# Layer 1's second product as seven products over two super-tiles, issued from a slot list

## The chip, the cores and the metric

The kernel runs on one core of a Trainium2 chip. The metric is device time in microseconds (us) from start to end of one execution; the median of several runs is given. Engines are called by the profile's names: PE (TensorE, matmuls), PEld (its weight loads), DVE (VectorE), ACT (ScalarE), POOL (GpSimd), SP (SyncE, which here only issues transfers).

## The reference, cut to what matters

Four layers are applied to `x` of shape 128 x 64 x 256, each `x = x + layer(relu(layernorm(x)))`: a graph convolution with LSTM windows (layer 0), a normalised graph convolution with an MLP (layer 1), a three-matrix graph convolution (layer 2) and masked attention (layer 3). The change is in layer 1:

```python
agg = jnp.einsum('nm,bmd->bnd', A_hat, features)
x = agg.reshape(-1, d)                              # 8192 x 256
h = jax.nn.relu(_batchnorm(x @ W1.T + b1, g1, be1)) # first product, 8192 x 512
out = h @ W2.T + b2                                 # second product, 8192 x 256
out = _batchnorm(out, g2, be2)
```

A batchnorm needs the mean and variance of each channel over all 8192 rows. So nothing of the second product can start before the first product is done for every row, and nothing of the next layer before the second is.

## The kernel before, in words

The 8192 rows are cut into 16 super-tiles of 512 rows (`SUP = 512`, `NS = 16`). All is float32. In layer 1 the data lie channel-major: a tile holds 128 channels on the partitions and the 512 rows of a super-tile along the free axis. The hidden 512 channels are four such chunks (`HC = 4`), the output's 256 are two (`KC = 2`).

The kernel runs in stages: layer 0's graph part; the LSTM; `first_product`; `second_product`; and `rest`, which holds layers 2 and 3. Where a stage goes through super-tiles, `pipelined` advances the generators of several super-tiles by one step in turn, the newest first, and this order is the order of each engine's queue (`tc.manual_schedule()`). Each engine works through its queue in order; semaphores make it wait for data.

The steps that the change touches:

- `zslot(s, c)` is the place of chunk c of super-tile s of the hidden layer. Chunks 0 and 1 lie in the large buffers `hbuf` (`hS`, `hT`), chunks 2 and 3 in the tiles `zb` (called `z` in the profile). The second product writes its output over chunks 0 and 1.
- `first_product(s)` loads x, copies layer 0's result in row order with POOL (`hs`, L330), transposes it on PE (L203) and adds x, applies the layernorm (whose power is one POOL operation, L179), aggregates over the graph on PE (L193), multiplies by W1 on PE (L341), evicts with the bias on ACT (L343) and takes statistics on DVE (L346).
- `bn_coeffs` turns the statistics of all super-tiles into one scale and one shift per channel (L580 to L585).
- `second_product(s)`, before: ACT applies scale, shift and Relu to four chunks in place (L618); PE sums four matmuls into each of two banks (L626); DVE adds the bias on the way out of PSUM (L630) and takes statistics (L631). One super-tile's Relus stand a step ahead of its matmuls.
- `rest(s)` loads layer 1's input again (`x1`, L662), applies the second batchnorm's coefficients to y (L665) and transposes back (L203).

The LSTM already uses a seven-product form. Each gate over two blocks of 512 columns is a 2 x 2 by 2 x 2 block product in seven products instead of eight, with three PSUM banks "a", "b" and "c", of which "a" is evicted and then accumulated into further. Its work is a list of events `at(t, fn, ...)`, sorted by t and issued in that order; t counts slots of PE time. The weight sums that the form needs come from `weight_sums`, on POOL; the input sums from DVE (`input_sums`, L385), the state sums from DVE or POOL (`state_sums`, L405 to L408). The weights lie in a tile of seven blocks, the last three or four of them made from the first four.

Of the kernel before, what the change touches and what calls it, by code (L numbers as in the profile page):

```python
# [9 lines left out]
F32 = mybir.dt.float32  # L10
AF = mybir.ActivationFunctionType
ALU = mybir.AluOpType
AX = mybir.AxisListType

P = 128
# [5 lines left out]
def kernel(ctx: ExitStack, tc: tile.TileContext, a: dict, out: bass.AP):  # L21
# [4 lines left out]
    nc = tc.nc  # L26
# [4 lines left out]
    KC = D // P  # L31
    SUP = 512
    NS = NT // SUP
# [6 lines left out]
    HC = H1 // P  # L40
# [27 lines left out]
    def bank():  # L68
        return psum.tile([P, 512], F32, tag="ps", name="ps")
# [12 lines left out]
    def weight(name, src, pool=const):  # L82
        k, m = src.shape
        return load_const(name, src.rearrange("(c p) m -> p c m", p=P), [P, k // P, m], pool)
# [24 lines left out]
    bn2 = load_const("bn2", a["bn2"], [P, 3, KC])  # L109
# [87 lines left out]
    def to_token_major(src, add, dst):  # L197

        for q2 in range(0, Q, 2):
            p_ = bank().rearrange("p (q d) -> p q d", q=2)  # L200
            for q in range(2):
                for c in range(KC):
                    nc.tensor.transpose(p_[:, q, ts(c, P)], src(c, q2 + q), ident)  # L203
            nc.vector.tensor_add(dst[:, q2 : q2 + 2, :], add[:, q2 : q2 + 2, :], p_)
# [6 lines left out]
    def place(s):  # L211
        return hbuf[s // SG], (s % SG) * SUP
# [7 lines left out]
    def pipelined(gens, skew, live=()):  # L220

        gens, live, r = list(gens), list(live), 0
        with tc.manual_schedule():
            while gens or live:
                if gens and r % skew == 0:
                    live.insert(0, gens.pop(0))
                live = [g for g in live if next(g, "end") != "end"]
                r += 1  # L230
# [12 lines left out]
    OF = (None, A11, A12, S4, A22, S1, S2, S3)  # L243
# [9 lines left out]
    def weight_sums(w):  # L253
        g = nc.gpsimd
        g.tensor_add(w[:, S1], w[:, A21], w[:, A22])
        g.tensor_sub(w[:, S2], w[:, S1], w[:, A11])
        g.tensor_sub(w[:, S3], w[:, A11], w[:, A21])
        g.tensor_sub(w[:, S4], w[:, A12], w[:, S2])
# [60 lines left out]
    def zslot(s, c):  # L319

        g, c0 = place(s)
        return g[:, c, c0 : c0 + SUP] if c < KC else zb[s][:, c - KC, :]

    def first_product(s):
        xt = pb[0].tile([P, Q, D], F32, tag="xt", name="xt")
        nc.sync.dma_start(xt, x_r[s])
        hs = pb[0].tile([P, KC * SUP], F32, tag="hs", name="hs")
        hsT = hs.rearrange("p (c n) -> p c n", c=KC)
        for c in range(KC):
            nc.gpsimd.tensor_copy(hsT[:, c, :].rearrange("p (b t) -> p b t", t=T), graphs(s, c))  # L330
        yield
        to_token_major(lambda c, q: hsT[:, c, ts(q, P)], xt, xt)
        nc.sync.dma_start(x1d[s], xt)
        h = layernorm_relu(lns, xt, h=hs.rearrange("p (q d) -> p q d", q=Q))
        yield
        ag = aggregate(pb[0], h, ahT, "ag", 2)
        yield
        for o in range(HC):
            p_ = bank()
            for c in range(KC):  # L340
                nc.tensor.matmul(p_, w1[:, c, ts(o, P)], ag[:, c, :],  # L341
                                 start=(c == 0), stop=(c == KC - 1))
            nc.scalar.activation(zslot(s, o), p_, AF.Identity, bias=bn1[:, 0, o : o + 1])  # L343
        yield
        for o in range(HC):
            nc.vector.bn_stats(st1[:, o, s, :], zslot(s, o))  # L346
        yield
# [7 lines left out]
    events = []  # L355

    def at(t, fn, *args):
        events.append((t, len(events), fn, args))
# [169 lines left out]
    t = 0.0  # L528
    wt[0][0].append(wih0[0])
    for p in range(1, NL + 1):  # L530
# [8 lines left out]
        for k in range(0, len(pairs), 2):  # L539
            sts = [{"blk": blk, "N": blk[0][2] * GB, "p": p, "pool": pool}  # L540
                   for blk, pool in zip(pairs[k : k + 2], (lh0, lh1))]
            for j in range(p):
                for st in sts:
# [4 lines left out]
                    t = step(t, st, j, j == p - 1, l, wt[l], turn)  # L548
# [40 lines left out]
    hbuf = [spare.tile([P, KC, GRP], F32, tag="hS", name="hS"), *hT]  # L589

    with tc.tile_pool(name="pz", bufs=1, reuse_waits="tile") as pz:
        w2 = weight("w2", a["W2T"], pz)
        zb = [pz.tile([P, HC - KC, SUP], F32, tag=f"z{s}", name=f"z{s}") for s in range(NS)]
        st1 = pz.tile([P, HC, NS, 6], F32, tag="st1", name="st1")
        st2 = pz.tile([P, KC, NS, 6], F32, tag="st2", name="st2")

        gens = [*early, *(first_product(s) for s in range(3, NS))]
        with tc.manual_schedule():
            next(gens[3])
            next(gens[0])  # L600
        pipelined(gens[4:], 1, gens[3::-1])
        front.close()
        last.close()
        late = ctx.enter_context(tc.tile_pool(name="late", bufs=1, side="right", reuse_waits="tile"))
        wl2 = [weight(f"wl2_{k}", a["W"][k], late) for k in range(3)]
        bl2 = row_bcast("bl2", a["bias"], D, late)
        wqk = late.tile([P, KC, D], F32, tag="wqk", name="wqk")
        wvo = late.tile([P, KC, D], F32, tag="wvo", name="wvo")
        products = ExitStack()
        wt = products.enter_context(tc.tile_pool(name="wt", bufs=1, reuse_waits="tile"))  # L610
        wqkv = weight("wqkv", a["Wqkv"], wt)
        wo = weight("wo", a["Wo"], wt)
        co1 = bn_coeffs(pz, st1, HC, bn1, "bn1")

        def second_product(s):
            for c in range(HC):
                z = zslot(s, c)
                nc.scalar.activation(z, z, AF.Relu, bias=co1[:, 1, c : c + 1],  # L618
                                     scale=co1[:, 0, c : c + 1])
            yield  # L620
            acc = []
            for o in range(KC):
                p_ = bank()
                acc.append(p_)
                for c in range(HC):
                    nc.tensor.matmul(p_, w2[:, c, ts(o, P)], zslot(s, c),  # L626
                                     start=(c == 0), stop=(c == HC - 1))
            for o in range(KC):
                y = zslot(s, o)
                nc.vector.tensor_scalar_add(y, acc[o], bn2[:, 0, o : o + 1])  # L630
                nc.vector.bn_stats(st2[:, o, s, :], y)  # L631
            yield

        pipelined(map(second_product, range(NS)), 1)
        co2 = bn_coeffs(pz, st2, KC, bn2, "bn2")

        with tc.manual_schedule():
            wT = wt.tile([P, 3 * KC, D], F32, tag="wT", name="wT")  # L640
            for k in range(3):
                p_ = bank().rearrange("p (d c) -> p d c", d=KC)
                for d in range(KC):
                    for c in range(KC):
                        nc.tensor.transpose(p_[:, d, ts(c, P)], wqkv[:, c, ts(k * KC + d, P)], ident)
                nc.scalar.copy(wT[:, k * KC : (k + 1) * KC, :], p_)
            for left, right, to in ((0, wT[:, KC : 2 * KC, :], wqk), (2, wo, wvo)):
                p_ = bank().rearrange("p (c m) -> p c m", c=KC)
                for c in range(KC):
                    for d in range(KC):  # L650
                        nc.tensor.matmul(p_[:, c, :], wT[:, left * KC + d, ts(c, P)],
                                         right[:, d, :], start=(d == 0), stop=(d == KC - 1))
                nc.scalar.copy(to, p_)
        products.close()


    with tc.tile_pool(name="pc", bufs=2, reuse_waits="tile") as pc, tc.tile_pool(name="pc1", bufs=1, reuse_waits="tile") as pc1:

        def rest(s):
            g, c0 = place(s)  # L660
            x1 = pc.tile([P, Q, D], F32, tag="x1", name="x1")
            nc.sync.dma_start(x1, x1d[s])  # L662
            y = g[:, :, c0 : c0 + SUP]
            for c in range(KC):
                nc.vector.tensor_scalar(y[:, c, :], y[:, c, :], co2[:, 0, c : c + 1],  # L665
                                        co2[:, 1, c : c + 1], op0=ALU.mult, op1=ALU.add)
            yield
            x2 = pc.tile([P, Q, D], F32, tag="x2", name="x2")
            to_token_major(lambda c, q: y[:, c, ts(q, P)], x1, x2)


            h = layernorm_relu(pc, x2)
# [4 lines left out]
            for c in range(KC):  # L677
                for q2 in range(0, Q, 2):
                    half = [bank()[:, : 6 * T].rearrange("p (q k n) -> p q k n", q=2, k=3)
                            for _ in range(2)]  # L680
                    for q in range(2):
                        for b in range(2):
                            r = slice(b * T, (b + 1) * T)
                            nc.tensor.matmul(half[b][:, q], h[r, q2 + q, ts(c, P)], adj3[r, :, r],  # L684
                                             start=True, stop=True)
                    for b in range(2):
                        copy = nc.vector.tensor_copy if b else nc.scalar.copy
                        to = ag[:, c, :, q2 * P : (q2 + 2) * P].rearrange("p k (q n) -> p q k n", q=2)
# [3 lines left out]
            for q2 in range(0, Q, 2):  # L692
                p_ = bank().rearrange("p (q d) -> p q d", q=2)
                for q in range(2):
                    for n in range(3 * KC):
                        c, k = divmod(n, 3)
                        nc.tensor.matmul(p_[:, q, :], ag[:, c, k, ts(q2 + q, P)], wl2[k][:, c, :],  # L697
                                         start=(n == 0), stop=(n == 3 * KC - 1))
# [6 lines left out]
            for c in range(KC):  # L705
                p_ = bank()
# [5 lines left out]
            for o in range(KC):  # L712
                p_ = bank()
                for c in range(KC):
                    nc.tensor.matmul(p_, wqk[:, c, ts(o, P)], h3T[:, c, :],  # L715
                                     start=(c == 0), stop=(c == KC - 1))
# [3 lines left out]
            p_ = bank()  # L720
            for q in range(Q):
                for c in range(KC):
                    nc.tensor.matmul(p_[:, ts(q, P)], qk[:, c, ts(q, P)], h3T[:, c, ts(q, P)],  # L723
                                     start=(c == 0), stop=(c == KC - 1))
# [76 lines left out]
```

## Time and profile before

| what | value |
|---|---|
| time, median of 3 runs | 1948.85 us (1948.57 to 1951.17) |
| span of the profiled run | 1946.4 us |
| PE busy | 1900.9 us (98%) |
| DVE busy | 1071.7 us (55%) |
| ACT busy | 830.3 us (43%) |
| POOL busy | 506.2 us (26%) |
| granted PE clock, mean | 0.996 |
| second product's matmuls (L626) on the final chain | 111.83 us, from 1392.81 |

PE, PEld and the others are separate rows: a PE that is busy says that matmuls are in its pipeline, and the row PEld, the weight loads, overlaps it. The chain that ended last is followed backwards from the last instruction, at each step to what released it; time on it is time that the kernel's end depends on. A single f32 matmul of the program is two MATMUL records and two LDWEIGHTS records in this trace. "Idle before" tells how long an engine stood still ahead of an instruction and who released it.

### The profile page before, as it was taken

How to read it: one execution, taken by the hardware profiler on the slowest of the kernel's cores; microseconds unless marked ns; L12 is line 12 of the kernel's file. 1: busy time of each engine (PE TensorE's matmuls, PEld its weight loads, DVE VectorE, ACT ScalarE, POOL GpSimd, SP SyncE). 2: the span in 40 equal slices, each digit the busy share in tenths (PEclk: the TensorE clock that was granted, in tenths of full speed). 3: DMA queues.
4: the chain of work that ended last, by engine and by line, in shares of the span. 5: the costliest groups of instructions: out<-in, count | busy, mean ns of one | idle time of the engine just before them, and what ended most of it. 6: DMA issues, size and time to landing. Idle time of an engine off the chain costs nothing.

```text
span 1946.4 us, 19096 instructions
## 1 busy us (share of the span) xinstructions
PE 1900.9 (98%) x7092; PEld 1156.7 (59%) x7092; DVE 1071.7 (55%) x2108; ACT 830.3 (43%) x1398; POOL 506.2 (26%) x330
## 2 busy tenths in 40 slices
PE   7999999999999999999999999999999899999998
PEld 6776444444446666665444444555444678888887
DVE  6775777635447345345433334688544555556553
ACT  3554667534435335335433333344650243333332
POOL 1110322543324434322522224432000211111110
PEclk9999999999999999999999999999999999999999
DMA  5110000000001000000000001333000101111111
GB/s 156 55 33 1 1 1 26 19 0 0 0 0 44 1 1 1 1 1 22 0 0 1 1 0 54 109 109 117 11 0 21 34 1 44 44 44 44 44 33 44
DMA packets 48909, 54.29 MB, mean 28 GB/s; under 512 B 2992, under 2 KB 44208, under 8 KB 48816
## 3 DMA queue, kind: packets, MB, share of 16 engines
q1 hardware_dynamic: 44784, 49.29, 7.9%
q10 hardware_dynamic: 4032, 3.78, 0.7%
q8 instruction: 56, 0.92, 0.2%
q14 instruction: 37, 0.30, 0.1%
HBM read 36.28 MB, written 16.78 MB: 27 GB/s over the span
## 4 chain that ended last, share of the span: by engine, by line
PE 94%; DVE 2%; ACT 1%; POOL 1%; DMA 1%; issue 0%; DVEq 0%; POOLq 0%; ACTq 0%
PE ps L423 33%; PE ps L429 18%; PE ps L697 9%; PE ps L626 6%; PE ps L341 6%; PE ps L193 5%; PE ps L753 3%; PE ps L289 3%; PE ps L300 3%; PE ps L715 2%; PE ps L684 2%; PE ps L723 1%; PE ps L203 1%; PE ps L745 1%; PE ps L708 1%; DVE ln_st L176 0%
## 5 line engine op out<-in xcount | busy, mean ns | idle before, releaser
L445 DVE TENSOR_TENSOR gate<-gate,ps 128x512 f32<-128x512 f32 (+2 forms) x378 | 223.7, 619 | 456.9 <-PE ps L429 377.4
L423 PE MATMUL ps<-tx,wih 128*128 128x512 f32 (+2 forms) x1008 | 448.4, 544 | 6.0 <-ACT gate L448 4.0
L423 PE MATMUL ps<-hT,wih 128*128 128x512 f32 (+2 forms) x756 | 338.5, 541 | 0.0
L423 PEld LDWEIGHTS ps<-tx,wih 128*128 128x128 f32 x1008 | 191.1, 191 | 196.9 <-issue 133.7
L448 ACT COPY gate<-ps 128x512 f32<-128x512 f32 (+2 forms) x252 | 134.2, 533 | 378.5 <-PE ps L429 324.6
L441 ACT ACTIVATE gate<-gate,lbias 128x512 f32<-128x512 f32 (+2 forms) x252 | 216.7, 860 | 153.6 <-DVE gate L445 153.6
L429 PE MATMUL ps<-h,whh 128*128 128x512 f32 (+2 forms) x576 | 257.5, 529 | 0.0
L423 PEld LDWEIGHTS ps<-hT,wih 128*128 128x128 f32 x756 | 143.6, 190 | 142.1 <-issue 79.9
L179 POOL TENSOR_TENSOR ln_rn<-ln_rn,mhalf 128x4 f32<-128x4 f32 x64 | 64.7, 1010 | 522.9 <-DVE ln_rn L178 522.9
L429 PE MATMUL ps<-th,whh 128*128 128x512 f32 (+2 forms) x432 | 192.5, 527 | 0.0
L429 PEld LDWEIGHTS ps<-h,whh 128*128 128x128 f32 x576 | 109.7, 191 | 100.6 <-issue 76.9
L697 PE MATMUL ps<-wl,ag 128*128 128x256 f32 x768 | 168.4, 379 | 0.0
L697 PEld LDWEIGHTS ps<-wl,ag 128*128 128x128 f32 x768 | 144.7, 190 | 19.0
L468 POOL TENSOR_TENSOR gate<-gate 128x1024 f32<-128x1024 f32 (+2 forms) x36 | 71.9, 2019 | 309.6 <-ACT gate L441 309.6
L183 ACT ACTIVATE ln_h<-x,ln_rn 128x256 f32<-128x256 f32 x128 | 66.4, 589 | 189.4 <-DVE ln_rn L180 189.4
L468 POOL TENSOR_TENSOR cell<-gate 128x1024 f32<-128x1024 f32 (+2 forms) x36 | 79.4, 2225 | 200.1 <-ACT gate L441 200.1
L429 PEld LDWEIGHTS ps<-th,whh 128*128 128x128 f32 x432 | 82.2, 190 | 75.9 <-issue 58.1
L341 PE MATMUL ps<-ag,w 128*128 128x512 f32 x256 | 112.3, 592 | 0.0
L468 POOL TENSOR_TENSOR cell<-gate,cell 128x1024 f32<-128x1024 f32 (+2 forms) x32 | 65.1, 2052 | 103.6 <-ACT gate L441 103.6
L448 DVE COPY gate<-ps 128x512 f32<-128x512 f32 (+2 forms) x126 | 78.5, 623 | 21.6 <-PE ps L429 21.6
L441 ACT ACTIVATE gate<-ps,lbias 128x512 f32<-128x512 f32 (+2 forms) x126 | 79.5, 631 | 3.5 <-PE ps L429 0.5
L473 ACT ACTIVATE gate<-cell 128x1024 f32<-128x1024 f32 (+2 forms) x72 | 68.2, 952 | 27.8 <-POOL cell L468 27.8
(164 smaller groups left out, 2492.8 us busy)
## 6 DMA issues: line engine op xcount, KB each, us to landing
xt<-in_x_dram SPq DMA_DIRECT2D x31, 512.0 KB, 4.4
x1d<-xt SPq DMA_DIRECT2D x16, 512.0 KB, 3.0
x<-x1d SPq DMA_DIRECT2D x16, 512.0 KB, 4.5
out_dram<-x SPq DMA_DIRECT2D x16, 512.0 KB, 3.2
wih<-in_WihT_dram SPq DMA_DIRECT2D x16, 256.0 KB, 4.8
whh<-in_WhhT_dram SPq DMA_DIRECT2D x12, 256.0 KB, 4.7
wqkv<-in_Wqkv_dram ACTq DMA_DIRECT2D x1, 768.0 KB, 4.3
wl<-in_W_dram ACTq DMA_DIRECT2D x3, 256.0 KB, 3.2
```

The lines of the kernel that those rows point to most:

```text
L183: nc.scalar.activation(h[:, q, :], src[:, q, :], AF.Relu, bias=rn[:, 1, q : q + 1], scale=rn[:, 0, q : q + 1])
L193: nc.tensor.matmul(p_[:, ts(q, P)], h[:, q, ts(c, P)], mT, start=True, stop=True)
L341: nc.tensor.matmul(p_, w1[:, c, ts(o, P)], ag[:, c, :], start=(c == 0), stop=(c == KC - 1))
L423: nc.tensor.matmul(wide(p_[:, :N]), wih[0][:, OF[k], gi, :], x_, start=first_, stop=(j == 0), skip_group_check=True)
L429: nc.tensor.matmul(p_[:, :N], whh[0][:, OF[k], gi, :], h_, start=False, stop=True, skip_group_check=True)
L441: nc.scalar.activation(to, r[bank_][:, :N] if bank_ else to, fn, bias=lbias[:, l, m : m + 1])
L445: nc.vector.tensor_add(slot(n, hc), slot(n, hc), r[bank_][:, :N])
L448: op(slot(n, hc), r[bank_][:, :N])
L468: fn(*((t["G"] if isinstance(t, dict) and "G" in t else st["c"])[:, n, :, : st["N"]] for t in tiles))
L473: nc.scalar.activation(o_, c, AF.Tanh)
L626: nc.tensor.matmul(p_, w2[:, c, ts(o, P)], zslot(s, c), start=(c == 0), stop=(c == HC - 1))
L697: nc.tensor.matmul(p_[:, q, :], ag[:, c, k, ts(q2 + q, P)], wl2[k][:, c, :], start=(n == 0), stop=(n == 3 * KC - 1))
```

## The change

Two neighbouring super-tiles are taken together. With rows n = 0, 1 (the super-tile) and, for each half k of the hidden channels, two chunks c = 0, 1, the product of the two by the weights is a 2 x 2 by 2 x 2 block product, summed over k = 0, 1. It is computed with seven block products per k instead of eight. This takes four sums of the weights, made once by POOL at `s == 8` of the first product (`weight_sums(w2)`), and four sums of the hidden chunks (T1 to T4) for each pair and k: those of k = 0 on DVE, those of k = 1 on POOL. T3 is made in place, over chunk b12; the rest lie in a new pool `tp` with two buffers. Three banks per pair, "a", "b", "c", are used as in the LSTM's gates: "a" is evicted by ACT after product 1, accumulated into by 6, evicted again, accumulated into by 7, added by DVE to y(1,1), accumulated into by 4 and evicted at last.

All is put on a slot list. Pair i starts at slot 7i and its products stand at 7i + 0, 1, 3, 5, 9, 11 and 13, so two pairs interleave and every slot has one product of two matmuls. The four outputs are written over chunks that are no longer needed, which permutes them over the pair; `yslot` tells where each lies, for the statistics and for `rest`. The bias is now added by ACT on three of the outputs' evictions and on that of "a" into T2. W2's tile grows from four blocks of 256 columns to seven blocks of 2 x 128 and is loaded in four pieces from SP, where it was one transfer from ACT's queue.

```diff
+    def yslot(s, o):
+        n, c = {(0, 0): (0, 0), (1, 1): (0, 1), (1, 0): (1, 1), (0, 1): (1, 0)}[s % 2, o]
+        return zslot(s - s % 2 + n, c)
...
     def first_product(s):
         xt = pb[0].tile([P, Q, D], F32, tag="xt", name="xt")
+        if s == 8:
+            weight_sums(w2)
...
-        w2 = weight("w2", a["W2T"], pz)
+        w2 = pz.tile([P, 7, 2, P], F32, tag="w2", name="w2")
+        for o in range(2):
+            for c in range(2):
+                nc.sync.dma_start(w2[:, 2 * o + c], a["W2T"].rearrange(
+                    "(k c p) (o m) -> o c p k m", c=2, p=P, m=P)[o, c])
...
-        def second_product(s):
-            for c in range(HC):
-                z = zslot(s, c)
-                nc.scalar.activation(z, z, AF.Relu, bias=co1[:, 1, c : c + 1],
...
-                for c in range(HC):
-                    nc.tensor.matmul(p_, w2[:, c, ts(o, P)], zslot(s, c),
-                                     start=(c == 0), stop=(c == HC - 1))
-            for o in range(KC):
-                y = zslot(s, o)
-                nc.vector.tensor_scalar_add(y, acc[o], bn2[:, 0, o : o + 1])
-                nc.vector.bn_stats(st2[:, o, s, :], y)
...
+            def sums(name, k, engine):
...
+                b11, b21, b12, b22 = (z(n, 2 * k + c) for n in range(2) for c in range(2))
+                if name == "T1":
+                    engine.tensor_sub(tt["T1"][:, k], b12, b11)
+                elif name == "T2":
+                    engine.tensor_sub(tt["T2"][:, k], b22, tt["T1"][:, k])
+                elif name == "T3":
+                    engine.tensor_sub(b12, b22, b12)
+                else:
+                    engine.tensor_sub(tt["T4"][:, k], b21, tt["T2"][:, k])
...
+            for k, (n, c) in enumerate(((0, 1), (0, 3), (0, 0), (0, 2), (1, 0), (1, 2), (1, 1), (1, 3))):
+                at((-6.3, -5.8, -5.3, -4.4, -3.9, -3.4, -2.4, -1.9)[k], relu, n, c)
+            for k, engine in enumerate((nc.vector, nc.gpsimd)):
+                for name, t in (("T1", -2.8), ("T2", 0.1), ("T3", 0.6), ("T4", 1.6)):
+                    at(t, sums, name, k, engine)
+            for t, name, j in ((0, "c", 2), (1, "a", 1), (3, "b", 5), (5, "a", 6), (9, "a", 7),
+                               (11, "b", 3), (13, "a", 4)):
+                at(t, product, name, j)
+            at(2, lambda: evict(y(0, 0), 0, "a"))
+            at(3.1, lambda: add(y(0, 0), y(0, 0), "c"))
+            at(3.6, stats, 0, 0)
+            at(4, lambda: evict(y(1, 1), 1, "b"))
+            at(6, lambda: evict(tt["T2"][:, 0], 0, "a"))
+            at(10, lambda: add(y(1, 1), y(1, 1), "a"))
+            at(10.5, stats, 1, 1)
+            at(12, lambda: add(y(1, 0), tt["T2"][:, 0], "b"))
+            at(12.5, stats, 1, 0)
+            at(14.2, lambda: evict(y(0, 1), 1, "a"))
+            at(15, stats, 0, 1)
...
         def rest(s):
-            g, c0 = place(s)
...
-            y = g[:, :, c0 : c0 + SUP]
+            y = [yslot(s, c) for c in range(KC)]
```

More of the change, by code (lines that the diff above doesn't have):

```diff
@@ L613 @@
         co1 = bn_coeffs(pz, st1, HC, bn1, "bn1")
-        def second_product(s):
-            for c in range(HC):
-                z = zslot(s, c)
-                nc.scalar.activation(z, z, AF.Relu, bias=co1[:, 1, c : c + 1],
-                                     scale=co1[:, 0, c : c + 1])
-            yield
-            acc = []
-            for o in range(KC):
-                p_ = bank()
-                acc.append(p_)
-                for c in range(HC):
-                    nc.tensor.matmul(p_, w2[:, c, ts(o, P)], zslot(s, c),
-                                     start=(c == 0), stop=(c == HC - 1))
-            for o in range(KC):
-                y = zslot(s, o)
-                nc.vector.tensor_scalar_add(y, acc[o], bn2[:, 0, o : o + 1])
-                nc.vector.bn_stats(st2[:, o, s, :], y)
-            yield
@@ L634, with second_product, z, relu @@
-        pipelined(map(second_product, range(NS)), 1)
+        events = []
+        def second_product(i, tp):
+            t0 = 7.0 * i
+            tt, banks = {}, {}
+            def z(n, c):
+                return zslot(2 * i + n, c)
+            def relu(n, c):
+                nc.scalar.activation(z(n, c), z(n, c), AF.Relu, bias=co1[:, 1, c : c + 1],
+                                     scale=co1[:, 0, c : c + 1])
+            def sums(name, k, engine):
+                if name != "T3" and name not in tt:
+                    tt[name] = tp.tile([P, 2, SUP], F32, tag=name, name=name)
+                b11, b21, b12, b22 = (z(n, 2 * k + c) for n in range(2) for c in range(2))
[7 more added lines that the diff above has]
+                    engine.tensor_sub(tt["T4"][:, k], b21, tt["T2"][:, k])
+            def product(name, j):
+                new = name not in banks
+                if new:
+                    banks[name] = bank()
+                for k in range(2):
+                    x_ = (z(0, 2 * k), z(0, 2 * k + 1), z(1, 2 * k + 1),
+                          *(tt[v][:, k] if v in tt else None for v in ("T4", "T1", "T2")),
+                          z(1, 2 * k))[j - 1]
+                    nc.tensor.matmul(banks[name], w2[:, OF[j], k, :], x_, start=(new and k == 0),
+                                     stop=(k == 1), skip_group_check=True)
+            def evict(to, o, name):
+                nc.scalar.activation(to, banks[name], AF.Identity, bias=bn2[:, 0, o : o + 1])
+            def add(to, src, name):
+                nc.vector.tensor_add(to, src, banks[name])
+            def y(n, o):
+                return yslot(2 * i + n, o)
+            def stats(n, o):
+                nc.vector.bn_stats(st2[:, o, 2 * i + n, :], y(n, o))
+            def at(t, fn, *args):
+                events.append((t0 + t, len(events), fn, args))
+            for k, (n, c) in enumerate(((0, 1), (0, 3), (0, 0), (0, 2), (1, 0), (1, 2), (1, 1), (1, 3))):
[17 more added lines that the diff above has]
+            at(15, stats, 0, 1)
@@ L635 @@
+        with tc.tile_pool(name="tp", bufs=2, reuse_waits="tile") as tp:
+            for i in range(NS // 2):
+                second_product(i, tp)
+            with tc.manual_schedule():
+                for _, _, fn, args in sorted(events, key=lambda e: e[:2]):
+                    fn(*args)
         co2 = bn_coeffs(pz, st2, KC, bn2, "bn2")
@@ L659, in rest @@
         def rest(s):
-            g, c0 = place(s)
             x1 = pc.tile([P, Q, D], F32, tag="x1", name="x1")
             nc.sync.dma_start(x1, x1d[s])
-            y = g[:, :, c0 : c0 + SUP]
+            y = [yslot(s, c) for c in range(KC)]
             for c in range(KC):
-                nc.vector.tensor_scalar(y[:, c, :], y[:, c, :], co2[:, 0, c : c + 1],
-                                        co2[:, 1, c : c + 1], op0=ALU.mult, op1=ALU.add)
+                nc.vector.tensor_scalar(y[c], y[c], co2[:, 0, c : c + 1], co2[:, 1, c : c + 1],
+                                        op0=ALU.mult, op1=ALU.add)
             yield
             x2 = pc.tile([P, Q, D], F32, tag="x2", name="x2")
-            to_token_major(lambda c, q: y[:, c, ts(q, P)], x1, x2)
+            to_token_major(lambda c, q: y[c][:, ts(q, P)], x1, x2)
             h = layernorm_relu(pc, x2)
```

## The prediction

> **What bounds the kernel now.** I read the page's engine shares first, then the chain by line, the chain in order of time, and then only the stage that the change touches.
>
> ```profile
> PE 1900.9 (98%) x7092; PEld 1156.7 (59%) x7092; DVE 1071.7 (55%) x2108; ACT 830.3 (43%) x1398; POOL 506.2 (26%) x330
> PE 94%; DVE 2%; ACT 1%; POOL 1%; DMA 1%; issue 0%; DVEq 0%; POOLq 0%; ACTq 0%
> ```
>
> PE carries 94% of the chain that ended last, so a PE instruction removed counts in full unless a wait takes its place. The chain in order of time shows how much of it is this stage:
>
> ```profile
> 1374.22 13.75 PE ps L341 x32
> 1392.81 111.83 PE ps L626 x256
> 1506.24 3.72 PE ps L651 x16
> 1516.18 4.54 PE ps L684 x32
> ```
>
> L626, the second product, is one unbroken block of 111.83 us. Its 256 records are 128 matmuls of the program: each f32 matmul leaves two. The windows (us, PE, PEld, DVE, ACT, POOL, granted clock, DMA) split that block:
>
> ```profile
> 1392.00:1400.00 8.00, 7.19 (x13) 3.12 (x14) 0.79 (x2) 8.00 (x12) 0.00 (x0) 0.79 0.00 0
> 1400.00:1420.00 20.00, 20.00 (x48) 8.80 (x47) 8.10 (x12) 20.00 (x29) 0.00 (x0) 1.00 0.00 1
> 1420.00:1505.00 85.00, 85.00 (x203) 37.84 (x202) 36.74 (x52) 17.17 (x25) 0.00 (x0) 1.00 0.00 0
> ```
>
> From 1400 on PE never idles, at full clock; POOL does nothing, DVE is busy 45 of 105 us, and ACT, which runs ahead with its Relus, is done by 1438. Matmul starts in the timeline are 1.717 us apart for four records, 0.429 each. 256 x 0.429 = 109.9, so 1.9 us of the 111.83 are lost at the start. The timeline there:
>
> ```profile
> 1391.95 1.52 ACT L618 ACTIVATE hS<-hS,bn1co 128x512 f32<-128x512 f32 x2 [3.26 <-DVE bn1co L585]
> 1394.20 0.34 PEld L626 LDWEIGHTS ps<-hS,w 128*128 128x128 f32 x1 [0.40 <-issue]
> 1397.19 0.19 PEld L626 LDWEIGHTS ps<-z,w 128*128 128x128 f32 x1 [0.24 <-issue]
> ```
>
> PE comes out of a 4.9 us idle spell and loads weights at 0.34 us, half speed, until about 1396.8: that is the loss. At the end of the stage:
>
> ```profile
> 1504.76 0.75 DVE L630 TENSOR_SCALAR hT<-ps,bn 128x512 f32<-128x512 f32 x1 [0.47 <-PE ps L626]
> 1505.54 0.69 DVE L631 BATCH_NORM_STATS2 st<-hT 128x6 f32<-128x512 f32 x1
> ```
>
> Behind these come the statistics, the coefficients and the first transposes of the last stage. PE's filler (L645, L651) lies beside them.
>
> **What the Trainium skill says.** "TensorE: Matmul & The Clock Gate", section What's actually happening: PE's clock is halved when idle and needs about 3.4 us of work to warm; the trace agrees (0.34 against 0.19 us for about 4 us). "SBUF — State Buffer", section Who interferes with whom: a VectorE instruction with two SBUF inputs contends with a GpSimd instruction that reads SBUF. The trace agrees: the L385 subtractions below go from 0.69 to 2.85 us. "PSUM — Partial Sum Buffer", section The four PSUM rules: a matmul without the first flag adds onto what the bank holds, which is what reusing bank "a" after an eviction rests on; the gates at L423 do the same here.
>
> **Prices.** From the traced lines (min/median/max) and groups (busy us, mean ns):
>
> ```profile
> L343 ACT ACTIVATE z<-ps,bn x32: 669/676/687, 1248.8 to 1388.0; 128x512 f32<-128x512 f32 x32
> L385 DVE TENSOR_TENSOR tx<-hT,tx x72: 478/692/2851, 187.9 to 1181.7; 128x512 f32<-128x512 f32 x48, 128x320 f32<-128x320 f32 x12, 128x352 f32<-128x352 f32 x12
> L407 POOL TENSOR_TENSOR h<-h 128x512 f32<-128x512 f32 x6 | 7.6, 1265 | 0.0
> L407 POOL TENSOR_TENSOR h<-h 128x352 f32<-128x352 f32 x2 | 1.9, 926 | 0.0
> ```
>
> **1. PE, removed.** A pair of super-tiles has 16 matmuls now and gets 7 products x 2 halves of the contraction = 14. Over 8 pairs that is 112 for 128: 32 records fewer, 32 x 0.429 = **-13.7 us**, all on the path. The stage's floor is 224 x 0.429 = 96.1 us, 12.0 per pair or 1.717 per slot.
>
> **2. Do the others keep up at 12.0 us a pair?** ACT: 8 Relus at 0.705 (start to start) and 4 evictions at 0.62 (L343, two in 1.24) = 8.1. DVE: 4 subtractions at 0.69, 3 additions from PSUM at 0.68 (L445), 4 statistics at 0.69 = 7.6 alone. POOL: 4 x 1.27 = 5.1. If each DVE subtraction also sits out a whole POOL one (1.27), DVE reaches 12.7; I take some collisions, about 9, since POOL is busy under half the time.
> The new waits, in slots of pair i: ACT waits for PE before its evictions at 2, 4, 6 and 14.2. Queued behind are pair i+1's Relus; modulo 7 the slots let ACT finish three Relus (1.2 slots) between evictions 1.8 to 2 slots apart, and pair i+1's last Relu ends at about 5.2, 1.8 slots before PE begins that pair. DVE waits for PE before y(1,1) at 10; behind it lie y(0,0), statistics and the next T1. PE needs the bank back only at 13, three slots (5 us) later. T1 is made at about 5 and used at 10, T2 before 7 and used at 12. Bank "a" must be evicted between 1 and 5 and between 5 and 9, with another pair's product between. Six of eight banks are live. Each hand-off has at least one slot, mostly three, against under 1 us: **0** in the steady part. The same arrangement for the LSTM gates runs gapless (188 to 365 us: PE busy 176.92 of 177.00), with DVE busy 132 us of it.
>
> **3. The start.** PE still starts after the first Relu, at 1392.8, and half clock covers slot 0 (four records at 0.86, to 1396.3). Slot 1 runs to 1398.0. Relu 5 ends at 1395.6 and relu 7 at 1397.1; T1 on POOL, 1396.3 to 1397.6, so slot 3 runs to 1399.7. Slot 5 adds onto "a" and waits for its eviction, which stands on ACT behind 11 Relus: 1391.95 + 11 x 0.705 = 1399.7, plus 0.68 = 1400.4. It ends at 1402.1; four full slots from 1392.8 would end at 1399.7. Loss 2.4 against 1.9 now: **+0.5** (0 to 1.5, if port collisions hold T2 up).
>
> **4. The end.** The last pair's slots 9, 11 and 13 stand alone, but 11 hides the addition that frees "a", and pair 6's slot 13 hides the eviction before 9. Then ACT's 0.68 replaces DVE's 0.75 ahead of the same 0.69 statistics: **0**.
>
> **5. The weight sums.** At s = 8 of the stage before, four POOL operations of 128x256 go ahead of the copies. The rows at 512 and 352 give 2.1 ns an element, so about 0.72 each, an estimate; 2.9 in all. Round 8 now:
>
> ```profile
> 1290.92 1.01 POOL L179 TENSOR_TENSOR ln_rn<-ln_rn,mhalf 128x4 f32<-128x4 f32 x1 [6.50 <-DVE ln_rn L178]
> 1291.88 2.08 POOL L330 COPY hs<-hT 128x512 f32<-128x512 f32 x2
> 1296.04 1.04 PE L203 MATMUL ps<-ident,hs 128*128 128x128 f32 x8
> ```
>
> POOL idled 6.5 us before the L179 of super-tile 6, but the sums are queued behind it, so that idle time doesn't help. The copies end at 1296.9 instead of 1294.0, and PE's transposes wanted them at 1296.0. PE is full there (136.00 of 136.00 us from 1251 to 1387), so **+0.9** (0 to 2) is lost. The next L179, at 1300.4, is clear of it.
>
> **6. The rest: 0.** W2's load, now four transfers on SP, can start when the last recurrent matmul frees its memory (about 1241), as before. At worst it holds x's fourth load from 1235.8 to about 1242.5, landing 4.4 later at 1246.9, before the addition at 1249.0; W2 is wanted 40 us later. The y's at other addresses are the same two operations in the last stage, and the permutation costs no copy.
>
> **Sum.** 1948.85 - 13.7 + 0.5 + 0.9 = **1936.5**.
>
> **Rivals.**
> A, 0.72: as worked out, 1935 to 1938.
> B, 0.18: a small wait per pair. For it: bank "a" changes hands three times a pair, and with every port collision DVE needs 12.7 for 12.0. Against: three slots of slack, and the gapless gates. 0.5 to 0.7 us x 8 = 4 to 5.6: about 1941.
> C, 0.06: the stage before loses more, for SP waiting on memory ahead of x's loads, or the sums and copies blocked by DVE. SP's later loads have some 3 us of slack; a 5 us stall gives 1941.5.
> D, 0.04, slower: the interleaving fails, since an instruction waiting for PE stands ahead of one that PE needs. Then slots 5, 9 and 13 each pay a hand-off of about 0.75 us: 3 x 0.75 x 8 = 18, or 1954.5. Against it: the slot list never puts a pair's need behind a later pair's product.
>
> **How the numbers follow.** The time is A's. Low is the full 13.7 with nothing given back, 1935.1, less the 0.3 by which runs undercut the median: 1934.8. High takes in most of B: 1941.0. 0.2% is 3.9 us, the line at 1944.95: A, nearly all of B and most of C lie below it, 0.92; 0.04 for a stall near 12 us that cancels the gain, 0.04 for D.
>
> **What would show it.** The second product's matmuls fall from 256 to 224 records and its block to about 98.6 us, with PE full from its tenth us on; ACT about 65 us busy in it, POOL about 41 from nothing. PE has one idle spell of about 1 us near 1296 before L203 and at most one near 1400. Wrong: a gap that repeats every 12 us (B), L203 gaps in other rounds (C), a stage of 110 us or more (D).

## The result, and the profile after

The changed kernel takes 1937.25 us (median of 4, 1936.99 to 1938.08) against 1949.23 us before (median of 4 runs by now, 1948.57 to 1951.17): 12.0 us less, ratio 0.9938 with a 95% interval of 0.992 to 0.9955. A second series gave 1935.62 (5 runs) against 1948.15 (25 runs): 12.5 us less, ratio 0.9935, interval 0.9923 to 0.9948. The forecast was 1936.5, and the range 1934.8 to 1941.0.

First the page's engine shares and the chain by engine:

```profile
PE 1890.1 (98%) x7060; PEld 1152.6 (60%) x7060; DVE 1099.9 (57%) x2132; ACT 852.1 (44%) x1430; POOL 557.4 (29%) x366
PE 93%; DVE 2%; issue 2%; ACT 1%; POOL 1%; DMA 1%; DVEq 0%; POOLq 0%; ACTq 0%
```

PE has 32 records fewer, DVE, ACT and POOL have 24, 32 and 36 more, and PE is still the bound. The chain in order of time (start, length, what; the second product is L663 now):

```profile
1395.32 7.60 PE ps L663 x12
1402.94 91.26 PE ps L663 x212
1497.25 6.55 issue
1505.73 4.45 PE ps L755 x32
```

The stage's matmuls begin at 1395.32 and end at 1402.94 + 91.26 = 1494.20: 98.88 us where it was 111.83, so **12.95 us** less. From the end of the block to the first matmul of layer 2 (L755) it is 11.53 us, which it was before to within a hundredth (1504.64 to 1516.18). The windows of the stage (us, PE, PEld, DVE, ACT, POOL, granted clock, DMA) show how full the other engines became:

```profile
1395.00:1403.00 8.00, 7.66 (x13) 3.05 (x13) 4.16 (x4) 8.00 (x13) 3.94 (x3) 0.70 0.00 0
1403.00:1494.20 91.20, 91.20 (x214) 40.45 (x215) 69.94 (x85) 57.38 (x83) 43.96 (x30) 1.00 0.00 1
```

PE is busy 91.20 of 91.20 us. DVE, which had 45 of 105 us before, is now busy 77% of the time and POOL 48%, both while PE hides them. The first 8 us run at a mean clock of 0.70.

The span of this profiled run is only 10.7 us shorter (1935.7 for 1946.4), since it was already 2.5 us late when the stage began. That lateness is no part of the change, as the first experiment shows.

### The profile page after: what moved, and what is told of

Read it like the earlier page. It is cut to its first block, busy times and chain, and to the rows that moved or that the text cites. A ratio compares the mean times of both kernels' runs of the same rounds, so it can differ in the third digit from the quotient of the medians.

```text
span 1935.7 us, 19149 instructions
## 1 busy us (share of the span) xinstructions
PE 1890.1 (98%) x7060; PEld 1152.6 (60%) x7060; DVE 1099.9 (57%) x2132; ACT 852.1 (44%) x1430; POOL 557.4 (29%) x366
## 4 chain that ended last, share of the span: by engine, by line
PE 93%; DVE 2%; issue 2%; ACT 1%; POOL 1%; DMA 1%; DVEq 0%; POOLq 0%; ACTq 0%
PE ps L430 33%; PE ps L436 19%; PE ps L768 9%; PE ps L663 5%; PE ps L348 5%; PE ps L193 5%; PE ps L824 3%; PE ps L289 3%; PE ps L300 3%; PE ps L786 2%; PE ps L755 2%; PE ps L816 1%; PE ps L794 1%; PE ps L203 1%; PE ps L779 1%
```

## The experiments

### The changed kernel once more

No edit.

> The changed kernel once more, to see what its profile repeats. Theory: the second product's block of matmuls is 96.1 us of matmuls (224 records at 0.429) plus about 2.7 us at half clock and small waits, so again 98.5 to 99.3 us, and the 2.5 us by which the first profile of the changed kernel ran late before this stage come from how long PE stays at half clock after idle spells and from the first microseconds, which vary from run to run. The time is then 11 to 13 us under the kernel before. Rival: the 2.5 us belong to the change (W2's loads on SP or the sums), and show again as the same lateness at the same places, 0.6 us by 188 us, 1.4 us more by 1234 us.

The second profile of the same kernel, the chain in order of time:

```profile
1400.49 91.26 PE ps L663 x212
1494.79 6.55 issue
1503.28 5.49 PE ps L755 x32
```

The block ends at 1491.75 and began at 1392.86: 98.89 us, and 11.53 us again to L755. The first product's matmuls start from 1241.6 to 1387.4 where the kernel before has 1241.5 to 1387.4: the 2.5 us are gone. So they came with that run and not with the change, and the rival falls. What varies from run to run is told at the end.

### The weight sums, with eight and with sixteen more

The diff is that of `sums_x3`; the second kernel, `sums_x5`, has 16 in place of 8.

```diff
         if s == 8:
             weight_sums(w2)
+            for _ in range(8):
+                nc.gpsimd.tensor_add(scratch, w2[:, A11], w2[:, A22])
```

> Eight further additions of the size of a weight sum stand behind the four at super-tile 8, 5.8 us more on POOL; their result is used by nothing. Theory of the prediction's step 5: the copies that follow feed the very next transposes, which have 2 us to spare, so PE loses 0.9 us with four sums and about 6.7 us here: the stage of the first product ends 5.8 us later than with four, and the time is 5.8 us over the changed kernel's. Rival theory, from the trace of after: the copies are wanted one round of 9.5 us later, and what comes first is the power of the layernorm behind them, ahead of which POOL still idles 3.5 us; the power then comes 2.3 us late, and PE, which wants its result 3 us later, loses nothing: same time as the changed kernel, within 0.5 us.

> Sixteen further additions, 11.6 us more on POOL. Step 5 of the prediction: 11.6 us more than the changed kernel. Rival theory: 3.5 us go into POOL's idle time and about 3 us into the slack between the Relus and PE's aggregation, so PE stands still for about 5 us once (4 to 6), and the time is 4 to 6 us over the changed kernel's.

First what the four sums alone do. The timeline of POOL and PE in the changed kernel:

```profile
1283.90 1.01 POOL L179 TENSOR_TENSOR ln_rn<-ln_rn,mhalf 128x4 f32<-128x4 f32 x1 [6.47 <-DVE ln_rn L178]
1284.87 0.72 POOL L255 TENSOR_TENSOR w<-w 128x256 f32<-128x256 f32 x1
1287.73 2.12 POOL L337 COPY hs<-hT 128x512 f32<-128x512 f32 x2
1289.02 1.04 PE L203 MATMUL ps<-ident,hs 128*128 128x128 f32 x8
1293.36 1.02 POOL L179 TENSOR_TENSOR ln_rn<-ln_rn,mhalf 128x4 f32<-128x4 f32 x1 [3.52 <-DVE ln_rn L178]
1298.55 1.04 PE L203 MATMUL ps<-ident,hs 128*128 128x128 f32 x8
```

The sums cost what was estimated (0.72 each, from 1284.87 to 1287.73 with POOL's order kept), and the copies end at 1289.85, after the transposes of 1289.02 have begun. Yet those did not wait: in the pipeline's order they belong to the super-tile before. The copies just made are read at 1298.55; `sums_x5` below, where the copies come late, shows it. What POOL's next idle time shows is 3.52 us where it was 6.5: the sums went into it.

With eight more, the time is 1936.86 us (4 runs, 1935.70 to 1938.61), 1.2 over the changed kernel's second series and inside the spread of the runs, where step 5 asks for 5.8. In its timeline POOL's idle time is used up, and PE's transposes still show no wait; only the aggregation behind them is a little late:

```profile
1283.37 6.38 POOL L334 TENSOR_TENSOR scratch<-w 128x256 f32<-128x256 f32 x8
1289.69 2.07 POOL L339 COPY hs<-hT 128x512 f32<-128x512 f32 x2
1291.73 1.02 POOL L179 TENSOR_TENSOR ln_rn<-ln_rn,mhalf 128x4 f32<-128x4 f32 x1
1294.18 1.04 PE L203 MATMUL ps<-ident,hs 128*128 128x128 f32 x8
1295.06 2.42 PE L193 MATMUL ps<-ahT,hs 128*128 128x128 f32 x16
```

L193 takes 2.42 us where it takes 1.95, and the starts of the first product's matmuls span 146.3 us (1239.7 to 1386.0) for 145.9. So eight more sums cost 0.4 to 0.5 us, where the rival theory said that PE loses nothing.

With sixteen more, PE stands still:

```profile
1296.16 2.01 POOL L339 COPY hs<-hT 128x512 f32<-128x512 f32 x2
1297.25 0.33 PE L203 MATMUL ps<-ident,hs 128*128 128x128 f32 x1 [2.80 <-POOL hs L339]
1298.23 0.98 PE L203 MATMUL ps<-ident,hs 128*128 128x128 f32 x7 [0.65 <-POOL hs L339]
1300.98 3.98 PE L193 MATMUL ps<-ahT,hs 128*128 128x128 f32 x16 [1.77 <-ACT hs L183]
```

The idle times are 2.80 + 0.65 + 1.77 = 5.2 us, as expected, but the cost is more: L193 then takes 3.98 us where it takes 1.95, so the clock is halved as well, and the starts of the first product's matmuls span 154.2 us (1239.8 to 1394.0): 8.3 more than the 145.9. The median is 11.9 over the second series (1947.49, 12 runs, 1944.69 to 1949.33). So the expectation of 4 to 6 us missed. The profiled run (1944.69) is the fastest of the twelve, at a mean clock of 0.992; the others have 0.989 to 0.992. More time at half clock would account for them, but only one of the twelve has a trace, so that is argued, not shown. That the median happens to lie at step 5's 11.6 doesn't save step 5: eight more sums cost 0.5 us where it asks for 5.8.

### An eighth product

```diff
+            at(13.7, product, "d", 4)
             at(2, lambda: evict(y(0, 0), 0, "a"))
```

> Each pair gets an eighth product of two matmuls into a bank of its own, read by nothing, with the operands of product 4. Theory: PE alone sets the stage, so 8 x 4 records x 0.429 = 13.7 us come back, the block is about 112.6 us and the time within 1 us of the kernel before. Rival: PE waits inside the stage (hidden in the busy figure), and an extra product fills part of those waits: less than 10 us come back.

1949.86 us (12 runs, 1948.76 to 1951.54): 14.2 over the changed kernel's second series, and 1.7 over the 1948.15 of the kernel before, where within 1 was expected. The line of its matmuls on the sums (min/median/max duration in ns, first and last start):

```profile
L663 PE MATMUL ps<-T,w x128: 592/592/697, 1397.6 to 1504.3; 128*128 128x512 f32 x128
```

The last starts at 1504.3 and ends 0.59 later; the block began at 1392.3, so it takes 112.6 us, as expected, 13.7 more than without. The extra product costs all of its matmul time. No wait inside the stage swallowed a part of it, and the stage is PE's alone.

### The pairs one after the other

```diff
-            t0 = 7.0 * i
+            t0 = 16.0 * i
```

> The pairs no longer interleave: pair i starts at slot 16i instead of 7i, so its seven products stand alone. Rival D of the prediction put a failed interleaving at three hand-offs of 0.75 us a pair: 18 us over the changed kernel, a block of about 117 us. Theory from the trace of after: only the eviction of bank a between products 6 and 7 has no other product beside it (the one before has product 5, the addition after 7 has product 3), so PE waits once a pair for about 0.8 us: 8 x 0.8 = 6 us over the changed kernel, a block of about 105 us. If PE never waits, interleaving is worth nothing.

1943.90 us (16 runs, 1942.78 to 1947.21): 8.3 over the changed kernel's second series where 6 was expected, and still 4.7 under the 1948.63 of the kernel before beside it (ratio 0.9978, 0.9971 to 0.9986). Chain, and timeline of the hand-off in pair 1:

```profile
1403.05 12.30 PE ps L663 x28
1416.12 12.30 PE ps L663 x28
1429.18 12.30 PE ps L663 x28
...
```

```profile
1415.38 0.69 ACT L667 ACTIVATE T<-ps,bn 128x512 f32<-128x512 f32 x1 [0.46 <-PE ps L663]
1416.12 1.12 PE L663 MATMUL ps<-hS,w 128*128 128x512 f32 x2 [0.78 <-ACT T L667]
```

A pair takes 13.06 us instead of 12.02. There is one wait, before product 7, for the eviction of "a" into T2, and no other; the view of waits names L667 seven times for PE and 5.7 us in all. The hand-off costs 1.04 us from start to start, not 0.78: the profile ends a matmul 0.59 us after its start, while the next could start after 0.43, so 0.16 is laid bare too, and the two records behind the wait take 1.12 us where two others take 1.02. The block runs from 1392.93 to 1499.92, 107.0 us where about 105 was expected: eight hand-offs of 1.04 and not of 0.8. Rival D's sum, three hand-offs of 0.75 us, was wrong in the count; even without interleaving the change would have been faster.

### All sums on DVE

```diff
-            for k, engine in enumerate((nc.vector, nc.gpsimd)):
+            for k, engine in enumerate((nc.vector, nc.vector)):
```

> DVE makes the sums of both halves k, POOL none. Theory: sums cost DVE 8 x 0.69 instead of 4 of 0.7 to 1.76, which they take now beside POOL's; DVE has 10.3 us of work a pair for PE's 12.0, so PE stays full, the time is that of the changed kernel within 0.7 us, and the mean DVE subtraction falls from about 1.26 us to 0.7. Rival (B of the prediction): DVE is close enough to the bound that 1 us more a pair shows as a wait at product 7 or 4, and the time rises by 4 us or more.

1936.08 us (4 runs, 1935.62 to 1937.23), the changed kernel's time. The groups of instructions, T3 made on DVE in the changed kernel (first fence) and in this one (second); the columns are busy us, mean ns, idle before:

```profile
L651 DVE TENSOR_TENSOR hT<-hT 128x512 f32<-128x512 f32 x6 | 10.5, 1750 | 0.0
L651 POOL TENSOR_TENSOR z<-z 128x512 f32<-128x512 f32 x8 | 13.7, 1714 | 0.0
```

```profile
L651 DVE TENSOR_TENSOR hT<-hT 128x512 f32<-128x512 f32 x6 | 4.1, 683 | 0.0
L651 DVE TENSOR_TENSOR z<-z 128x512 f32<-128x512 f32 x8 | 5.5, 683 | 0.0
```

Beside POOL's subtraction, DVE's takes 1.75 us instead of 0.68, and POOL's 1.71 instead of 1.27: both pay. Over all four sums DVE's mean is 1.28 us with POOL's help and 0.68 without. In windows of the stage after its start, DVE is busy 69.94 of 91.20 us with four sums and 69.73 of 91.30 with all eight. Sharing the sums with POOL spared DVE nothing here. The time doesn't tell the two apart, since PE hides either.

### The start: filler early, and the order of two evictions

The filler is the weight products of layer 3 (wqk, wvo), which occupy PE for some 5 us after the second product. `filler` puts them ahead of it. `filler_evict` also moves one eviction of the first pair:

```diff
+        made = []
+        with tc.manual_schedule():
+            wT = wt.tile([P, 3 * KC, D], F32, tag="wT", name="wT")
...
+                made.append((to, p_))
         co1 = bn_coeffs(pz, st1, HC, bn1, "bn1")
...
-            at(2, lambda: evict(y(0, 0), 0, "a"))
+            at(2 if i else 1.1, lambda: evict(y(0, 0), 0, "a"))
...
+            for t, (to, p_) in zip((6.1, 6.2), made):
+                events.append((t, len(events), nc.scalar.copy, (to, p_)))
```

> The weight products of the last stage that fill PE's idle time at the end of this stage (16 f32 transposes and matmuls, some 5 us) move ahead of it, into PE's 4.9 us idle spell, and their last two evictions to slot 6 of the list. If the loss at the start is PE's half clock, it falls from 2.7 us to under 1 us, and the time by 1.5 to 2 us, less the 0.4 us by which the filler may overrun. If the loss is that product 6 waits for an eviction behind 11 Relus, which needs 8.4 us from the first Relu whatever PE's clock, the clock only changes which wait is seen: the fifth slot still ends about 10.1 us after the first Relu began, as it does now (10.3), and the time stays within 0.5 us of the changed kernel's.

> As the last, and the first pair's first eviction of bank a goes ahead of two of the next pair's Relus (slot 1.1 instead of 2, for that pair alone). If half clock and this eviction share the loss, only both together take it away: the fourth product of the first pair ends about 8.5 us after the first Relu began instead of 10.3, and the time falls by 1.3 to 2 us under the changed kernel's. If it is neither (T2 on POOL comes too late), nothing falls.

The changed kernel's timeline at the start, to compare with:

```profile
1394.45 0.81 ACT L639 ACTIVATE hS<-hS,bn1co 128x512 f32<-128x512 f32 x1 [3.27 <-DVE bn1co L592]
1398.89 0.34 PEld L663 LDWEIGHTS ps<-hS,w 128*128 128x128 f32 x1 [0.52 <-issue]
1399.74 0.20 PEld L663 LDWEIGHTS ps<-z,w 128*128 128x128 f32 x1 [0.52 <-ACT hS L639]
1402.22 0.67 ACT L667 ACTIVATE hS<-ps,bn 128x512 f32<-128x512 f32 x1
1404.76 1.02 PE L663 MATMUL ps<-hS,w 128*128 128x512 f32 x2
```

`filler` takes 1937.31 us (5 runs, 1937.07 to 1937.40), `filler_evict` 1935.34 (5 runs, 1932.92 to 1936.01). The timelines of the same spot, `filler` first:

```profile
1392.47 0.82 ACT L655 ACTIVATE hS<-hS,bn1co 128x512 f32<-128x512 f32 x1 [1.81 <-DVE bn1co L592]
1400.25 0.67 ACT L683 ACTIVATE hS<-ps,bn 128x512 f32<-128x512 f32 x1
1400.97 1.98 PE L679 MATMUL ps<-T,w 128*128 128x512 f32 x4 [1.63 <-ACT hS L683]
```

```profile
1391.99 0.81 ACT L655 ACTIVATE hS<-hS,bn1co 128x512 f32<-128x512 f32 x1 [1.82 <-DVE bn1co L592]
1399.08 1.98 PE L679 MATMUL ps<-T,w 128*128 128x512 f32 x4 [0.22 <-ACT hS L683]
1400.90 1.02 PE L679 MATMUL ps<-hS,w 128*128 128x512 f32 x2
1405.16 1.12 PE L679 MATMUL ps<-hS,w 128*128 128x512 f32 x2 [0.67 <-ACT T L683]
```

In the changed kernel the fourth product ends at 1404.76, 10.31 us after the first Relu began at 1394.45, with PE at half clock until 1399.74. In `filler` PE is at full clock from the first matmul and the fourth product ends at 1402.79, 10.32 us after the first Relu: PE waits 1.63 us for the eviction of "a", which stands behind 11 Relus (ACT starts it at 1400.25). A wait that half clock had covered has come out, and nothing is won. With the eviction two Relus earlier too, the fourth product ends 8.91 us after the first Relu, for about 8.5 expected; but PE then waits 0.67 us for the next eviction in ACT's queue, and of 1.4 us only 0.5 is left at the end of the stage. The gain of 1.3 to 2 us that was expected isn't there.

### The second eviction too, with and without the filler

```diff
-            at(6, lambda: evict(tt["T2"][:, 0], 0, "a"))
+            at(6 if i else 5.02, lambda: evict(tt["T2"][:, 0], 0, "a"))
...
+                late = 1.5 if i == 1 and k > 5 else 0
-                at((-6.3, -5.8, -5.3, -4.4, -3.9, -3.4, -2.4, -1.9)[k], relu, n, c)
+                at((-6.3, -5.8, -5.3, -4.4, -3.9, -3.4, -2.4, -1.9)[k] + late, relu, n, c)
```

> As the last (filler early, the first pair's first eviction of a two Relus earlier), and the first pair's second eviction of a, into T2, goes ahead of the second pair's last two Relus. Theory: in the first 14 us ACT's queue sets PE's pace, 16 Relus and three evictions in line, and the trace of the last run shows the wait moved from product 6 to product 7, about 0.9 us, for that second eviction; here it is gone too. The second product's matmuls then end about 98.4 us after the first Relu began, where the changed kernel needs 99.75 and the last run 99.3, and the time is 1 to 1.5 us under the changed kernel's, near 1934.3. Rival: the wait moves on again, to the sums of the second pair, and nothing more falls.

> Only the two evictions are moved, the filler stays at the end. Theory: PE is at half clock for its first 4.4 us and finishes the second product only 6.6 us after the first Relu began, so the eviction can't be much earlier; the fourth product ends about 10.0 us after it instead of 10.3 and the gain is 0.3 us, nothing that can be measured. If more than 1 us falls, half clock has no part in it.

`filler_order` takes 1935.89 us (5 runs, 1934.42 to 1936.99), `order_only` 1936.49 (5 runs, 1932.18 to 1937.07). The chains, in the same order:

```profile
1399.42 91.27 PE ps L679 x212
```

```profile
1394.63 98.57 PE ps L663 x224
```

The block of `filler_order` ends at 1490.69, 98.4 us after its first Relu (1392.3), as expected: the stage is 1.4 us shorter than the changed kernel's 99.75. The time, expected near 1934.3, doesn't show it: the medians of these kernels lie between the changed kernel's own two. `order_only` ends at 1493.20, 99.4 after its first Relu (1393.8), 0.3 less, as expected; its chain has no wait in the 98.57 us, so what it has over 96.1 is half clock and the last matmul's tail. No version is shown to be faster than the change.

## Why the prediction was right, and where it was not

**The bound** (PE alone in this stage) held: an eighth product costs its full matmul time.

**Step 1** (32 records, 13.7 us, all on the path) is shown by the block, 111.83 to 98.88 with the start's part in it, and by the eighth product, which brought 13.7 back.

**Step 2** (the others keep up, 0) is right: 91.20 busy of 91.20 us. DVE's instructions come to 9.9 us a pair (four subtractions at 1.28, three additions at 0.69, four statistics at 0.69) where about 9 were taken. POOL has 6.0 (47.9 over 8 pairs) where 5.1 were taken: the prediction let only DVE pay for collisions, but POOL pays too, 1.71 for 1.27. Both stay within 12.0, and no wait shows in the steady part. ACT's 66.7 us met the 65.

**Step 3** (the start, +0.5 within 0 to 1.5) measured +0.8: the block is 2.8 us over its 96.1 where before it was 1.9 over 109.9. The mechanism was the one named. The fourth product ended 10.31 us after the first Relu in both profiles, for 10.15 worked out; the eviction behind 11 Relus is what holds it at that, as `filler` shows at full clock. How the loss splits varies: the second profile has the 1.7 us of half clock and the 0.7 of waiting that were worked out, the first 2.2 and 0.3. The missing 0.3 is two terms of 0.16: the later end of the fourth product, and a sum that compared unlike things, for the 1.9 of before contains the last matmul's tail (0.59 us against 0.43 between starts) and the 2.4 does not.

**Step 4** (the end, 0): 11.53 us in both profiles, as before.

**Step 5** (the weight sums, +0.9) failed. It set the sums in front of the copies at 1291.88 and took the transposes at 1296.04 for their readers. Counted from the first, those copies are super-tile 9's, read at 1305.57. The copies of super-tile 8, behind the sums, stand one round earlier in the trace of before:

```profile
1282.35 2.08 POOL L330 COPY hs<-hT 128x512 f32<-128x512 f32 x2
```

They end at 1284.43 and are read at 1296.04, because the generator yields between copy and transposes and these follow a round later. So the slack was 11.6 us and not 2.1: the copies were read one round off. Four sums cost nothing, twelve about 0.5 us, and twenty, which outlast the slack, 8.3 us of the stage. The idle spell of about 1 us near 1296 that was to show the loss didn't occur, and the term was 0.9 us too large.

**Step 6** (the rest, 0): W2's four loads went out on SP at 1245.55, after the last recurrent matmul and after x's load at 1237.83, and the starts of the first product's matmuls span 145.9 us before and after.

With the terms as measured, 13.7 less 0.8 is 12.9 us off the stage; the times give 12.0 and 12.5, with runs of one kernel several us apart. The forecast of 12.3 came out as close as it did because its two errors partly cancelled, 0.9 too much given back in step 5 and 0.3 too little in step 3; that part is luck.

**The rivals.** B (a wait in every pair) didn't occur, nor C. D was priced at three hand-offs a pair; the serial kernel has one, of 1.04 us. With that one hand-off it isn't slower: with no interleaving at all the kernel is still 4.7 us faster than before. D's other ground, a queue that blocks PE because a wait stands ahead of what PE needs, didn't occur; what it would cost was not measured.

## What to carry to other kernels

A product form with fewer matmuls pays in full where PE is shown full and the added sums and evictions fit, per unit of PE time, on each other engine with their collisions counted; here 12 us of PE per pair held 10 of DVE, 8 of ACT and 6 of POOL. Before costing a delay on a queue, find the delayed tile and its reader by their index in the trace, and don't take the nearest pair of that kind: in a pipeline of generators either may be a round away. A bank that is evicted and used again needs another product beside the hand-off (1.04 us a pair without it here), and when one wait at a start is removed, ask which one stands behind it.

## What the runs showed of the hardware that was not expected

The kernel before, run 55 times beside these experiments, takes 1946.1 to 1951.1 us, and the mean granted PE clock sorts them: 1946.1 to 1946.5 at 0.997 (5 runs), 1946.2 to 1948.3 at 0.996 (22), 1948.0 to 1949.5 at 0.995 (20) and 1950.5 to 1951.1 at 0.994 (8). In the profile that ran late, PE stayed longer at half clock after its idle spells around 1202 and 1240 us. After the idle spell at the start of this stage it was 4.0 us from PE's first weight load until the loads were fast again in the kernel before and 4.4 us in the changed one's first profile; over all the runs in which PE idled there it was 3.4 (`sums_x3`) to 5.8 (`sums_x5`). The Trainium skill ("TensorE: Matmul & The Clock Gate", What's actually happening) gives about 3.4 and says that the window runs free, which fits a length that varies. The traces' clock records agree: every stretch at half clock that isn't cut off by the end of the run is 3.41, 6.83, 10.24 or 13.65 us long, multiples of one length, with the idle part in it. So two runs of one kernel can differ by some 1.7 us (half of 3.4) at each idle spell, an estimate: the first matmuls of layer 2 took 4.45 us in the first profile and 5.49 in the second. A difference of 1 us can't be read from a few times of this kernel, only from the stage in the trace.

Where DVE and POOL each subtract two SBUF tiles at once, neither simply blocks for the other's whole length: 0.68 and 1.27 us alone became 1.75 and 1.71 together, where one after the other would end at 1.95.
